# 115 products with no reader, put into half of TensorE's long planned waits

## The chip, the cores and the metric

The kernel runs on one core of a Trainium2 chip. The core has five engines that run their own instruction queues side by side: TensorE (PE: matrix products, and PEld: its weight loads), VectorE (DVE), ScalarE (ACT), GpSimd (POOL) and SyncE (SP, which here issues DMAs). Products land in PSUM, which has banks of 512 fp32 columns on 128 partitions. The metric is the device time of one execution in microseconds; the kernel before is given as the median of nine runs.

## The reference

The input `u` is 8 sequences of 512 tokens with 128 features. Four residual layers follow one another:

```python
x = u
x = x + ssm(layernorm(x))        # tanh/softplus gates, scan over time: z = a*z + b*u_scaled
x = x + linear(layernorm(x))     # one of 8 weight matrices, picked by argmax of logits + Gumbel noise
x = x + delta(layernorm(x))      # 16 heads of size 8, for each t: S += beta*(v - S k) k^T ; o = S q
x = x + moe(layernorm(x))        # 8 experts, top 2 by softmax weight, gelu(x w1 + b1) w2 + b2
```

The delta layer as it stands in the reference is a scan over time, also with a residual of its own inside (it returns `x + scan_out @ w_out + b_out`):

```python
def step(S, inp):
    q_t, k_t, v_t, beta_t = inp
    retrieval = jnp.einsum('bhij,bhj->bhi', S, k_t)
    S = S + jnp.einsum('bhi,bhj->bhij', beta_t * (v_t - retrieval), k_t)
    o_t = jnp.einsum('bhij,bhj->bhi', S, q_t)
    return (S, o_t)
```

## The kernel before, in words

Time is cut into 32 tiles of 16 steps (`QT = 16`); a tile holds 8 sequences x 16 steps = 128 tokens. Eight chunks `g` of four tiles each go through the front layers (`scanned`, `ssm_out`, `linear`, in `first_layers`), through the preparation of the delta rule (`delta_in`), the delta rule itself (`delta_rule`), and the routing (`route`). Groups of one or two chunks (`GROUPS`) then go through the experts (`experts`): tokens are scattered to a table in DRAM by GpSimd (`places`), blocks of 128 rows with one expert each are multiplied by `w1b` into bank `ph`, put through Gelu on ScalarE into `hid`, multiplied by `w2` into a bank `po` or `in`, and gathered back.

The delta rule is the serial part. A tile has four blocks of four steps. For each block VectorE does six instructions in a chain: a multiply of `kq` with the state into `so`, a reduction of `so` into `w`, a multiply with `tmat` into `prod`, a reduction of `prod` into `u_16`, a multiply of keys with it into the block's terms, and a reduction of these into the new state. The state lives in PSUM, in two banks of its own, `st[0]` and `st[1]`, which alternate from block to block; VectorE writes the state after block `n` into the bank of block `n + 1`. In each bank the state and its terms take columns 0 to 319 and `w` columns 320 to 351; `st[1]` also holds `u_16` in columns 352 to 479. Columns 352 to 511 of `st[0]` hold nothing. Before the change only VectorE writes these two banks; ScalarE reads `u_16` into `upd`. Once at the start VectorE clears both.

What each tile's rule needs comes from the other engines: `tmat` and the planes `qkp` from `delta_in`, by products with `head_ones` on TensorE, copies by ScalarE and small steps by GpSimd; `kq` by a DMA from a scratch in DRAM. At the end of a tile TensorE multiplies the planes of `so` and `qkp` with `wo`, and VectorE adds the result to `base`.

PSUM has eight banks here: `st0`, `st1`, `ph0`, `ph1` and four shared ones, `po0`, `po1`, `in0`, `in1`.

All work is recorded first, by `Recorder`, as operations of a `Plan` with an estimated cost each (`_cost`). `place` puts them in order: for each engine in turn it picks among the operations that are ready, by start and by due time, and notes a planned start and end. `best` tries 150 drafts (`DRAFTS`), with due times shaken at random from a fixed seed, and keeps the order with the earliest planned end. `emit` then issues the operations in that order, which the engines' queues keep: each engine executes its own in the order of issue. Semaphore waits between the engines are put in afterwards, from what each operation reads and writes, in the order of issue. `make_identity` writes `ident`, a 128 x 128 identity matrix in SBUF, before the plan's first operation.

In the profile most lines read L317, the line of the recorder's helper; the second product of the experts is L1300, the scatter L1238. So the groups are told apart by tile names.

Of the kernel before, what the change touches and what calls it, by code (L numbers as in the profile page):

```python
# [17 lines left out]
P = 128  # L18
# [52 lines left out]
class Plan:  # L71
# [41 lines left out]
    def add(self, engine, emit, reads, writes, cost, lag=0.0, table=None, group=None):  # L113
        op = Op()
        op.engine, op.emit, op.cost, op.lag, op.table = engine, emit, cost, lag, table
        op.key, op.slack = (self.key, len(self.ops)), self.slack
        op.after, op.begins, op.ends = set(), [], []
        for x in reads:
            self.depend(op, x, False)
        for x in writes:  # L120
            self.depend(op, x, True, group)
        for x in (*reads, *writes):
            if isinstance(x, Bank):
                if x.owner.users == 0:
                    op.begins.append(x.owner)
                if x.owner not in op.ends:
                    x.owner.users += 1
                    op.ends.append(x.owner)
        self.ops.append(op)
# [5 lines left out]
    def later(self, op, f):  # L135
# [4 lines left out]
        if f.engine != op.engine or op.lag < 0:  # L140
            wait += LAG[op.engine] + f.slack
        return wait
# [41 lines left out]
    def best(self):  # L184


        dice, kept = random.Random(1), None
        for draft in range(DRAFTS):
            if draft < len(SWITCH):
                due = {op.key[0]: op.key[0] for op in self.ops}  # L190
                self.switch = SWITCH[draft]
            else:
                due, self.switch = dict(kept[3]), kept[4]
                for key in due:
                    if dice.random() < MOVED:
                        due[key] += dice.gauss(0.0, JITTER)
            for op in self.ops:
                op.rank = due[op.key[0]]
            for turn in range(ROUNDS + 1):
                if turn:  # L200
                    self.backward()
                order, index = self.place()
                end = max(op.end for op in self.ops)
                if kept is None or end < kept[0]:
                    kept = end, order, index, due, self.switch
        for bank, i in kept[2].items():
            bank.index = i
        return kept[1]

    def place(self):  # L210
# [14 lines left out]
        while len(order) < len(self.ops):  # L225
# [40 lines left out]
            for b in op.ends:  # L266
                users[b] -= 1
                if users[b] == 0:
                    banks[index[b]] = done + LAG[op.engine]
            for f in followers[op]:  # L270
                at = done
                if f.engine != op.engine or op.lag < 0:
                    at += LAG[op.engine] + f.slack
                f.ready = max(f.ready, at)
# [4 lines left out]
        return order, index  # L279

    def emit(self):
        kind = mybir.EngineType
        with self.tc.manual_schedule(engines={kind.PE, kind.DVE, kind.Activation, kind.SP}):
            for op, switch in self.best():
                if switch:
                    self.hw.scalar.preload_act_table_set(switch)  # L286
                made = op.emit()
                if op.engine == "gpsimd":
                    self.tc.keep_in_program_order(made)


class Recorder:
# [5 lines left out]
    def __getattr__(self, name):  # L298
        plan, engine = self.plan, self.engine

        def record(*args, group=None, cost=None, **kw):
            def walk(x):
                if isinstance(x, bass.IndirectOffsetOnAxis):
                    return [x.ap]
                return [x] if isinstance(x, (bass.AP, Bank)) else []

            named = [k for k in ("out", "dst", "accum_out") if k in kw]
            outs = [a for k in named for a in walk(kw[k])]
            if not named or named == ["accum_out"]:
                outs += walk(args[0])  # L310
            ins = [a for x in (args if named[:1] in (["out"], ["dst"]) else args[1:]) for a in walk(x)]
            ins += [a for k, x in kw.items() if k not in named for a in walk(x)]

            def emit():
                on = lambda x: x.on(plan.banks) if isinstance(x, Bank) else x
                method = getattr(getattr(plan.hw, engine), name)
                return method(*(on(x) for x in args), **{k: on(x) for k, x in kw.items()})  # L317

            table = next((SETS[x] for x in args if isinstance(x, AF) and x in SETS), None)
            sizes = [_size(x) for x in outs + ins if not isinstance(x, Bank)]  # L320
            n = max([f for _, f in sizes], default=512)
            if "dma" in name:
                whole = min(p * f for p, f in sizes[:2]) if "indirect" not in name else sizes[0][0] * sizes[0][1]
                took, lag = (1.27 if engine == "gpsimd" else 0.42), -4.0 * whole
            else:
                took, lag = _cost(engine, name, n, kw), 0.0
                if ALU.pow in args:
                    took = 0.4 + 0.155 * n
            plan.add(engine, emit, ins, outs, took if cost is None else cost, lag, table, group)
# [32 lines left out]
MOVED = .2  # L362
ROUNDS = 1
LAG = {"tensor": 0.4, "vector": 0.3, "scalar": 0.3, "gpsimd": 0.3, "sync": 0.3}
SWITCH = (3.0, 6.0, 9.0, 12.0)


@with_exitstack
def seq_kernel(
# [42 lines left out]
    hw = tc.nc  # L412
# [22 lines left out]
    def bank(name):  # L435
        return psum.tile([P, N], F32, tag=name, name=name)

    shared = [bank(f"po{i}") for i in range(2)] + [bank(f"in{i}") for i in range(2)]
    nc = Plan(tc, shared)
    own = {t: [bank(f"{t}{i}") for i in range(n)] for t, n in (("ph", 2),)}  # L440

    def ctile(shape, name, dtype=F32):
        return const.tile(shape, dtype, tag=name, name=name)
# [101 lines left out]
    ident = ctile([P, P], "ident")  # L545
# [62 lines left out]
    st = [bank(f"st{i}") for i in range(2)]  # L608
# [8 lines left out]

    u_16 = st[1][:, NS + B * BL : NS + 5 * B * BL].rearrange("p (b t) -> p b t", b=B)

    nc.vector.memset(st[0], 0.0)  # L620
    nc.vector.memset(st[1], 0.0)

# [444 lines left out]
    def route(g, x3, group):  # L1067
# [27 lines left out]
        stat = stile([P, most], "stat")[:, 0:NT]  # L1095
        prob = stile([P, most, NE], "prob")[:, 0:NT]
        by.tensor_sub(prob, best, best[:, :, 0:1].to_broadcast([P, NT, NE]))
        nc.scalar.activation(prob, prob, AF.Exp)
        nc.vector.tensor_reduce(stat, prob, AX.X, ALU.add)
# [480 lines left out]
```

## Time and profile before

| what | value |
|---|---|
| median of 9 runs | 702.34 us (698.95 to 706.26) |
| profiled execution | 703.51 us |
| its span, first to last instruction | 701.7 us |
| mean granted TensorE clock | 0.856 |
| busy: PE, PEld | 513.3 us, 399.1 us |
| busy: DVE, ACT, POOL | 507.5, 458.6, 548.0 us |
| matmul records | 2948 |
| `so<-kq,st`, 128 times | 87.7 us, 685 ns each |

The busy time of an engine is the time in which it executes something, as a share of the span; matmuls are pipelined, and their ends are modelled. The page's second part cuts the span into 40 slices of 17.5 us and gives the busy tenths of each engine, and in the row PEclk the clock that TensorE was granted, in tenths of its full speed. The chain is followed back from the last instruction: at each step to what released it, or to the instruction ahead of it on its engine. In the order of time each row has the start, the duration, the engine, the line, the operation, what it writes and reads, and in brackets the idle time ahead of it with what ended that. In a row of several instructions (x8) the duration runs from the first start to the last end.

### The profile page before, as it was taken

Reading aid. Unit: us, or ns where it says so; the run is one execution under the profiler, and the core shown is the slowest. Engines: PE = TensorE matmul, PEld = TensorE weight load, DVE = VectorE, ACT = ScalarE, POOL = GpSimd, SP = SyncE. Lnnn points to the kernel's source line nnn. Section 1 sums busy time; section 2 is a strip of 40 time slices with the busy share of each in tenths; the row PEclk is TensorE's granted clock in tenths of the full one; section 3 lists DMA queues with packets and bytes.
Section 4 is the critical chain, followed back from the end, with each engine's and each line's share of the span. In section 5 each row is a group of like instructions: output and inputs, shape, how many; then the busy total and the mean of one; then the engine's idle time right before and its main releaser. Section 6 shows DMA issues by size and latency. Waiting matters only on the chain.

```text
span 701.7 us, 10975 instructions
## 1 busy us (share of the span) xinstructions
PE 513.3 (73%) x2948; PEld 399.1 (57%) x2948; DVE 507.5 (72%) x1276; ACT 458.6 (65%) x1054; POOL 548.0 (78%) x681
## 2 busy tenths in 40 slices
PE   5885564766675487788867878739888697897980
PEld 4563123534444245567645666639668687897980
DVE  5673179999999889999989999957999985400013
ACT  4866775756674668897877878736675544664750
POOL 7577575788589979997899998985799888884454
PEclk9957577897787579899988999979899989998995
DMA  3493053253245364655647566554878768568762
GB/s 106 130 284 96 24 133 81 78 150 71 76 98 150 79 187 108 156 151 159 190 119 180 132 175 162 143 165 141 216 204 222 188 192 245 140 198 233 207 192 74
DMA packets 97714, 105.92 MB, mean 151 GB/s; under 512 B 9099, under 2 KB 72534, under 8 KB 97654
## 3 DMA queue, kind: packets, MB, share of 16 engines
q1 hardware_dynamic: 92992, 96.66, 51.3%
q0 software_dynamic: 4160, 8.53, 4.4%
q8 instruction: 25, 0.41, 0.2%
q14 instruction: 35, 0.29, 0.1%
q10 hardware_dynamic: 502, 0.03, 0.0%
HBM read 81.26 MB, written 23.94 MB: 150 GB/s over the span
## 4 chain that ended last, share of the span: by engine, by line
DVE 37%; PE 20%; POOL 19%; ACT 9%; issue 9%; DMA 4%; SPq 1%; POOLq 0%; DVEq 0%; ACTq 0%
DVE st L317 18%; DVE so L317 6%; PE in L317 6%; PE ph L317 6%; PE po L317 4%; POOL b L317 3%; PE po L1300 3%; DVE prod L317 3%; POOL places L1238 3%; POOL f L317 2%; POOL back L317 2%; ACT f L317 2%; DVE x L317 2%; ACT b L317 2%; POOL so L317 2%
## 5 line engine op out<-in xcount | busy, mean ns | idle before, releaser
L317 ACT ACTIVATE hid<-ph,w1b 128x128 f32<-128x128 f32 x396 | 114.1, 377 | 54.2 <-PE ph L317 28.3
L317 PE MATMUL ph<-xbT,w1b 128*128 128x128 f32 x792 | 116.0, 291 | 17.3 <-ACT hid L317 5.8
L317 PEld LDWEIGHTS ph<-xbT,w1b 128*128 128x128 f32 x792 | 106.2, 206 | 25.1 <-ACT hid L317 7.0
L1300 PE MATMUL po<-w_sb,hid 128*128 x632 | 94.6, 289 | 9.9 <-ACT hid L317 7.3
L1300 PEld LDWEIGHTS po<-w_sb,hid 128*128 128x128 f32 x632 | 84.7, 201 | 24.2 <-issue 10.8
L317 DVE TENSOR_TENSOR so<-kq,st 128x512 f32<-128x512 f32 x128 | 87.7, 685 | 9.6 <-PE po L317 3.6
L317 DVE TENSOR_REDUCE st<-so 128x32 f32<-128x288 f32 x128 | 84.2, 658 | 3.3
L317 POOL DMA_INDIRECT back<-results,small_dest x64 | 62.1, 970 | 30.4 <-issue 13.7
L1238 POOL DMA_INDIRECT places<-xne,small_dest x64 | 64.5, 1007 | 19.1 <-issue 13.1
L317 PE MATMUL po<-wo,so 128*128 128x128 f32 x264 | 45.8, 329 | 32.5 <-POOL so L317 14.0
L317 PEld LDWEIGHTS po<-wo,so 128*128 128x128 f32 x264 | 42.8, 240 | 46.8 <-POOL so L317 15.1
L317 DVE TENSOR_REDUCE st<-st 128x64 f32<-128x320 f32 x128 | 63.8, 498 | 4.3
L317 PE MATMUL in<-b,head_ones 128*128 128x512 f32 x80 | 49.6, 709 | 14.9 <-DVE x L317 3.7
L286 ACT ACT_TABLE_LOAD x44 | 56.5, 1283 | 6.1 <-DMA hid<-in_L_ffn_b_dram 5.3
L317 DVE TENSOR_TENSOR st<-kq,st 128x256 f32<-128x256 f32 x128 | 54.8, 428 | 4.2
L317 PE MATMUL in<-b,wqkvb 128*128 128x512 f32 x64 | 44.6, 792 | 13.2 <-DVE x L317 5.4
L317 DVE SCALAR_TENSOR_TENSOR fin<-back,small_weight,fin 128x128 f32<-128x128 f32 x16 | 5.3, 352 | 61.9 <-DMA results<-yb 60.0
L317 PE MATMUL in<-f,wT 128*128 128x512 f32 x64 | 41.3, 735 | 7.4 <-ACT f L317 5.3
L317 POOL TENSOR_TENSOR qkp<-qkp,upd 128x512 f32<-128x512 f32 x32 | 38.9, 1217 | 7.7 <-ACT upd L317 7.5
L317 DVE TENSOR_REDUCE st<-prod 128x32 f32<-128x128 f32 x128 | 37.7, 294 | 7.0 <-ACT upd L317 1.2
L317 POOL TENSOR_TENSOR f<-f,f 128x512 f32<-128x512 f32 x24 | 30.7, 1282 | 12.9 <-ACT f L317 12.9
L317 DVE TENSOR_TENSOR prod<-tmat,st 128x128 f32<-128x128 f32 x128 | 36.6, 286 | 4.3
(287 smaller groups left out, 1242.8 us busy)
## 6 DMA issues: line engine op xcount, KB each, us to landing
kq<-scratch SPq DMA_DIRECT2D x64, 512.0 KB
w1b<-w1b_dram SPq DMA_DIRECT2D x99, 258.0 KB
xb<-places SPq DMA_DIRECT2D x21, 256.0 KB
results<-yb SPq DMA_DIRECT2D x21, 256.0 KB
places<-yb SPq DMA_DIRECT2D x2, 1472.0 KB
x<-in_L_attn_u_dram SPq DMA_DIRECT2D x32, 64.0 KB
w1b_dram<-in_L_ffn_w_dram SPq DMA_DIRECT2D x1, 2048.0 KB
scratch<-qn SPq DMA_DIRECT2D x8, 256.0 KB
```

The lines of the kernel that those rows point to most:

```text
L286: self.hw.scalar.preload_act_table_set(switch)
L317: return method(*(on(x) for x in args), **{k: on(x) for k, x in kw.items()})
L1238: rows_out = hw.gpsimd.indirect_dma_start(out=table[0 : nblk * P, :], out_offset=bass.IndirectOffsetOnAxis(ap=at, axis=0), in_=src, in_off ...
L1300: return hw.tensor.matmul(out_.on(nc.banks), lhsT=src, rhs=w2_f[:, bass.ds(at + c * P, P)], start=(c == 0), stop=(c == NHB - 1),)
```

## The change

`best` keeps, beside the order, each operation's planned start and end. When `emit` comes to a TensorE operation whose planned start lies more than 1.5 us (`GAP`) behind the planned end of the TensorE operation before it, it first issues some extra products: half of the wait (`FILL`) divided by 0.3 us (`FILLER`), rounded down. Over the whole plan these are 115. Each has one column of `ident` as its stationary operand and all of `ident` as its moving one, and writes one row of 128 columns (384 to 511) of `st[0]`, which nothing reads. The extra products are not operations of the plan: the plan's order, its times and the assignment of banks stay as they are.

```diff
                 if kept is None or end < kept[0]:
                     kept = end, order, index, due, self.switch
+                    self.times = {op: (op.start, op.end) for op, _ in order}
...
     def emit(self):
-        kind = mybir.EngineType
+        kind, free = mybir.EngineType, None
         with self.tc.manual_schedule(engines={kind.PE, kind.DVE, kind.Activation, kind.SP}):
             for op, switch in self.best():
+                if op.engine == "tensor":
+
+                    start, end = self.times[op]
+                    if free is not None and start - free > GAP:
+                        for _ in range(int(FILL * (start - free) / FILLER)):
+                            self.filler()
+                    free = end
...
+GAP, FILL, FILLER = 1.5, 0.5, 0.3
...
+    junk = st[0][0:1, 512 - P : 512]
+    nc.filler = lambda: hw.tensor.matmul(junk, lhsT=ident[:, 0:1], rhs=ident, start=True, stop=True)
     nc.vector.memset(st[0], 0.0)
     nc.vector.memset(st[1], 0.0)
```

## The prediction

> **What bounds the kernel now.** I read the page first: the slices, then the chain of work that ended last.
>
> ```profile
> span 701.7 us, 10975 instructions
> ...
> DVE  5673179999999889999989999957999985400013
> ...
> PEclk9957577897787579899988999979899989998995
> ...
> DVE 37%; PE 20%; POOL 19%; ACT 9%; issue 9%; DMA 4%; SPq 1%; POOLq 0%; DVEq 0%; ACTq 0%
> ```
>
> A slice is 17.5 us. From about 100 us to 590 us VectorE is nearly always full, and it holds the largest share of the chain: that is the delta rule (lines `st`, `so`, `prod`), a serial recurrence. TensorE holds a fifth of the chain. Its granted clock is low mostly in the first half. Next, busy time by stretch:
>
> ```profile
> core 0: us, PE busy (x) PEld busy (x) DVE busy (x) ACT busy (x) POOL busy (x), PEclk, DMA share, GB/s
> ...
> 52.00:105.00 53.00, 32.81 (x79) 13.79 (x79) 21.27 (x48) 39.27 (x63) 36.34 (x48) 0.69 0.33 87
> 105.00:290.00 185.00, 119.91 (x512) 80.59 (x512) 169.39 (x390) 123.24 (x221) 148.57 (x187) 0.80 0.43 110
> 290.00:420.00 130.00, 106.25 (x605) 80.60 (x604) 119.44 (x285) 104.68 (x226) 119.05 (x146) 0.89 0.59 158
> 420.00:702.00 282.00, 216.46 (x1604) 194.58 (x1602) 163.04 (x422) 159.71 (x452) 208.77 (x243) 0.91 0.66 183
> ```
>
> Between 105 and 290 VectorE works 169 of 185 us, TensorE 120. So TensorE's time is cheap there and VectorE's is dear. Before 105, where no delta rule runs yet, no engine is full and the chain hops between them; one stretch of it runs wholly at half clock:
>
> ```profile
> 62.90:90.20 27.30, 16.36 (x31) 6.72 (x31) 3.38 (x5) 19.14 (x35) 17.82 (x22) 0.50 0.12 32
> ```
>
> The last view is the order of time, for two things. First, one product's price at half and at full clock, from two rows of eight records, which are four products each (an fp32 product leaves two records; the page has 792 for the 396 products of `ph`):
>
> ```profile
> 66.49 2.08 PE L317 MATMUL in<-wsel,f 128*128 128x128 f32 x8 [0.68 <-ACT f L317]
> ...
> 654.89 1.06 PE L317 MATMUL ph<-xbT,w1b 128*128 128x128 f32 x8
> ```
>
> Second, what a reader of a PSUM bank waits for. The four products of one `hid` write four disjoint quarters of bank `ph`, and the first Gelu reads only the first quarter:
>
> ```profile
> 640.06 1.91 PE L317 MATMUL ph<-xbT,w1b 128*128 128x128 f32 x8
> ...
> 642.06 1.14 ACT L317 ACTIVATE hid<-ph,w1b 128x128 f32<-128x128 f32 x4 [6.69 <-PE ph L317]
> ```
>
> It starts at 642.06, 0.09 us after the last of the four (641.97), not after the first, though ScalarE had been idle for 6.69 us. In this program waits are placed by bank, not by column.
>
> **The change, part by part.** *Where the products go.* The plan's own start and end times (used here for order alone, not for time) have 28 TensorE waits over 1.5 us, 77.6 us in sum; half of each, cut into 0.3 us and rounded down, is 115 products. Nine waits with 48 products begin before the delta rule is two tiles old (plan 52.9 to 120.1), sixteen with 57 lie between 146 and 284, three with 10 at 362, 366 and 409. None lies in the last 290 us.
>
> *What each does.* It loads one column of `ident`, streams `ident`'s 128 columns and writes row 0, columns 384 to 511, of `st[0]`. No row shows a one-column load. The cheap end is 0.22 us, from the chain's piece of 16 back-to-back records at 575.73 (1.79 us); the dear end is 0.52, the half-clock row. I take 0.265 at full clock and 0.52 at half, from the two rows above, since there too the loads run beside the matmuls.
>
> *What waits for what.* `st[0]` is the bank in which the delta rule keeps its state. By the row above, a product waits for the last VectorE instruction on `st[0]` that stands ahead of it in the plan's order, and VectorE's next one on `st[0]` waits for the last product of the group. A group is emitted after everything planned to start before the TensorE instruction behind the wait, so the VectorE instruction ahead of it is one that starts just before the wait ends: the products run at the end of the wait, not in it. The tenth group, four products ahead of the `head_ones` product at 148.24, shows it:
>
> ```profile
> 148.24 1.10 PE L317 MATMUL in<-b,head_ones 128*128 128x512 f32 x2 [0.26 <-ACT f L317]
> ...
> 150.93 0.43 DVE L317 TENSOR_TENSOR st<-kq,st 128x256 f32<-128x256 f32 x1
> 151.39 0.50 DVE L317 TENSOR_REDUCE st<-st 128x64 f32<-128x320 f32 x1
> ```
>
> Today TensorE runs 2.7 us ahead of the plan's place here. Then the group waits until 151.36, and the reduction of 151.39 waits for four products.
>
> *VectorE's price.* I laid all 28 groups against the trace in this way. In seven, VectorE's next instruction on `st[0]` follows at once, and the group's time goes into the recurrence (the clock is that granted at that place):
> - 4 products behind 99.95, next 100.66, half clock: 2.08
> - 4 behind 150.93, next 151.39, full: 1.06
> - 4 behind 163.08, next 163.80, half; 0.43 us of other VectorE work lies between: 1.65
> - 4 behind 171.44, next 171.91, full: 1.06
> - 3 behind 287.31, next 288.03, half: 1.56
> - 4 behind 369.78, next 370.37, half: 2.08
> - 3 behind 372.71, next 373.17, half: 1.56
>
> That is 11.05 us, and two handovers of 0.09 us each time, less the usual 0.03 between two VectorE instructions: 7 x 0.15 = 1.05. Sum +12.1; with all at full clock 7.5. Six of the seven lie where the chain is VectorE's own; at 287 it runs through ScalarE and the transposes at 286.44, which would wait for the same group until about 289.7 instead, so that place pays either way. In the other seventeen groups after 97 us the next `st[0]` instruction is 1.5 to 4.3 us off, and the recurrence's work on the other bank covers the products; without it they would cost 0.265 to 0.52 each. At half clock the two groups of seven (behind 110.39 and 123.23, next 112.94 and 126.33) would overrun by 1.6 together, which goes to the range; the six behind 233.14 overrun where the chain is GpSimd's. The four groups at the front come below.
>
> *TensorE's own delay.* The product behind each such group starts late against VectorE: by 6 us at 96.40 (its group waits for the `so` multiply of 99.95), 4 at 148.24, 3 at 169.99 and 226.00, 1 to 2 elsewhere. Queued behind it are all later products, ScalarE's copies and GpSimd's steps on them. I cost it at nothing: after 96.40 TensorE has waits of 1.58 and 3.69, ScalarE of 2.51 and 4.48, GpSimd of 3.84 before the end of tile 0. Without that cover it costs what is left of the delay; the nearest limits are `tmat`, ready 2.57 us before its multiply at 156.91, and the linear layer's product, 0.74 us before the add at 168.65. From 0 to +6.
>
> *The clock.* Before the delta rule `st[0]` is free, and 25 products (3, 6, 12, 4) really run in waits, ahead of 59.78, 64.18, 73.67 and 79.69. The low stretches last multiples of 3.41 us. The one from 62.93 follows a 3.41 us in which TensorE worked 1.1 us; six products would make that 2.7. If they count as work, the transposes at 64.18 take 0.73 (the row at 113.88) instead of 1.63, the `wsel` products about 0.5 less, and the `head_ones` product at 79.69 takes 1.12 (57.88) instead of 2.08, with ScalarE idle behind it: -2.4. The rest of 73 to 85 is covered by ScalarE, busy without a break. If they do not count, 12 products at 0.52 end at 74.8 and 4 at 80.4, past the 73.67 and 79.69 they stand before: +1.8. I take -2.4, since every low stretch of this trace up to 690 us ends after 3.41 us in which TensorE worked over 2.8. In the delta rule I expect no gain: the products come when the wait is nearly over, and TensorE idles first as before.
>
> [...]
>
> **Sum.** +12.1 - 2.4 = +9.7. The profiled execution took 703.51 with a span of 701.7; the median of nine is 702.34. The change is added to the median: 712.0.
>
> **Rivals.**
> - *No wait on the bank* (faster): tracking by column lets the products run in the waits. For it: nobody reads those columns. Against: 642.06. Only the clock's 2.4 remains, up to 5 if later stretches profit: 697 to 700. It decides if VectorE's rows show no new wait.
> [...]
> - *The delay spreads*: ScalarE and GpSimd, held behind late products, keep VectorE waiting once more: +4 to +8, 716 to 720. For it: the 0.74 us. Against: the waits at 105 to 114.
>
> **How the numbers follow.** Forecast 0.60 (707 to 716: bounds 7.5 and 12.1, -2.4 and +1.8), spread 0.22, clock repays 0.10, no wait 0.08. A measurement tells about 0.3% (2.1 us) from no change. Faster: 0.08 and a third of the clock's case, 0.11; same, half of that case and 0.01 of the forecast, 0.06; slower 0.83. The range leaves out most of the no-wait case and the far end of the spread: 702 to 720.
>
> **What would show it.** VectorE waits of 1 to 2 us, ended by TensorE on `st`, at the seven places; TensorE waits ended by VectorE before the new rows; the products of the first four groups inside waits, and PEclk above 0.50 between 63 and 80. VectorE's busy time must stay at 507 us. It is wrong if the new rows start right behind the TensorE row ahead of them in the delta rule, or if GpSimd's chain at 200 to 240 does not move with VectorE's.

## The result and the profile after

The changed kernel takes 708.25 us (median of 10 runs, 705.56 to 714.2), the kernel before in the same comparison 702.33 us (31 runs). The ratio on record is 1.0109 with a 95% interval of 1.0082 to 1.0136, that is +7.7 us (5.8 to 9.6); the two medians lie 5.9 us apart, at the lower end of that. The change makes the kernel slower, by an amount that is known to about 2 us. The profiled execution took 708.48 us with a span of 706.8; before it was 703.51 and 701.7. TensorE's mean granted clock rose from 0.856 to 0.884 while the time grew.

The page of the changed kernel: the span, the slices of VectorE and of the granted clock, the chain by engine, and the group of the products (the helper's line is now L325, the products are L630).

```profile
span 706.8 us, 11448 instructions
...
DVE  5673159988899789899997999975999996300013
...
PEclk9957868898897599999998999988998999999995
...
PE 8%; DVE 3%; DMA 2%; issue 1%; POOL 1%; ACT 1%; POOLq 0%; SPq 0%; ACTq 0%; DVEq 0%
...
L630 PE MATMUL st<-ident 128*1 128x128 f32 x230 | 41.2, 341 | 42.7 <-DVE st L325 28.4
```

All 230 records of the 115 products are there. They keep TensorE busy for 41.2 us, and TensorE sits idle 42.7 us ahead of them, 28.4 of it for VectorE's work on `st`. The chain of this page is followed back only over a sixth of the span (its shares sum to 16%), so its shares can't be set beside those of before. VectorE's row is still nearly full from 100 to 590 us. Its busy time went from 507.5 to 505.2 us.

Busy time by stretch, the same stretches and columns as in the prediction, and the low-clock stretch of the front:

```profile
52.00:105.00 53.00, 37.05 (x128) 17.33 (x128) 20.45 (x44) 36.08 (x60) 33.77 (x46) 0.76 0.36 92
105.00:290.00 185.00, 137.99 (x653) 87.96 (x653) 165.37 (x386) 119.34 (x215) 146.16 (x180) 0.83 0.41 107
290.00:420.00 130.00, 100.29 (x619) 74.15 (x618) 117.27 (x284) 105.92 (x223) 117.87 (x151) 0.97 0.56 150
420.00:702.00 282.00, 223.48 (x1633) 201.37 (x1633) 168.67 (x435) 164.78 (x467) 215.09 (x248) 0.92 0.69 188
...
62.90:90.20 27.30, 19.82 (x81) 9.30 (x79) 4.32 (x8) 20.50 (x36) 17.63 (x22) 0.81 0.10 29
```

Between 105 and 290 TensorE works 18 us more and VectorE 4 us less (165.4 for 169.4): VectorE's missing time is new idle time. The clock rose in every stretch, most between 62.9 and 90.2, from 0.50 to 0.81.

The waits by who waits for whom (engine, tile, releaser: sum in us, times, longest):

```profile
PE st L630 <- DVE st L325: 28.4, 15, 5.0
...
DVE st L325 <- PE st L630: 10.1, 9, 2.0
```

The kernel before has neither. The second line, with one more wait of 1.5 us ahead of a multiply into `so`, is what the change makes VectorE wait: ten waits, 11.65 us. The first place of the seven shows it in the order of time:

```profile
102.48 0.68 DVE L325 TENSOR_TENSOR so<-kq,st 128x512 f32<-128x512 f32 x1
103.21 1.87 PE L630 MATMUL st<-ident 128*1 128x128 f32 x8 [6.94 <-DVE so L325]
105.00 2.08 PE L325 MATMUL in<-wT,f 128*128 128x128 f32 x8
105.11 0.66 DVE L325 TENSOR_REDUCE st<-so 128x32 f32<-128x288 f32 x1 [1.96 <-PE st L630]
```

VectorE's multiply ends at 103.16; four products (eight records) start 0.05 us later, after TensorE has been idle for 6.94 us. VectorE's reduction starts 0.03 us after the last of them and has waited 1.96 us. Before, it followed the multiply at once. The products write columns that no one reads; both engines wait all the same.

Where in the profile the time is lost and won can be followed by one and the same VectorE instruction in each trace. The table gives its start, as a difference to the kernel before (worked out from the orders of time; the four kernels of the right ran on one chip):

```
start before, and what it is             after   seven_only  without_seven  own_bank  one_each
 59.52  x<-in,gain,x (no product yet)    +2.8    +1.1        -1.0           -0.7      -1.3
 91.98  b<-b,beta                        +1.7    +1.1        -3.4           +0.2      -1.3
 99.95  first so<-kq,st                  +2.5    +1.3        -0.9           +0.6      -1.4
171.44  st<-kq,st                        +7.4    +6.4        -1.0           +0.7      +0.1
250.61  so<-kq,st                        +6.0    +6.4        -2.8            0.0       0.0
306.05  st<-prod                         +6.1    +6.3        -3.8           +1.9      -0.5
369.78  st<-st                           +3.9    +5.6        -4.3           +1.1      -1.6
535.19  st<-so                           +7.3    +9.1        -4.2           +2.2      -0.3
```

The first row stands ahead of every product, so its -1.3 to +2.8 is what two executions differ by at the start; a row is to be read against it.

### The profile page after: what moved, and what is told of

Read it like the earlier page. It is cut to its first block, busy times and chain, and to the rows that moved or that the text cites. A ratio compares the mean times of both kernels' runs of the same rounds, so it can differ in the third digit from the quotient of the medians.

```text
span 706.8 us, 11448 instructions
## 1 busy us (share of the span) xinstructions
PE 536.1 (76%) x3178; PEld 410.3 (58%) x3178; DVE 505.2 (71%) x1276; ACT 456.9 (65%) x1054; POOL 547.5 (77%) x681
## 5 line engine op out<-in xcount | busy, mean ns | idle before, releaser
L325 ACT ACTIVATE hid<-ph,w1b 128x128 f32<-128x128 f32 x396 | 113.9, 376 | 53.4 <-PE ph L325 25.1
L325 PE MATMUL ph<-xbT,w1b 128*128 128x128 f32 x792 | 115.4, 290 | 11.1 <-DMA w1b<-w1b_dram 4.2
L325 PEld LDWEIGHTS ph<-xbT,w1b 128*128 128x128 f32 x792 | 105.5, 205 | 19.1 <-ACT hid L325 6.0
L1311 PE MATMUL po<-w_sb,hid 128*128 x632 | 93.1, 286 | 8.4 <-ACT hid L325 6.2
L1311 PEld LDWEIGHTS po<-w_sb,hid 128*128 128x128 f32 x632 | 83.2, 198 | 21.5 <-issue 9.9
L325 DVE TENSOR_TENSOR so<-kq,st 128x512 f32<-128x512 f32 x128 | 87.7, 685 | 8.5 <-PE st L630 1.5
L325 DVE TENSOR_REDUCE st<-so 128x32 f32<-128x288 f32 x128 | 84.3, 659 | 6.1 <-PE st L630 2.9
L325 POOL DMA_INDIRECT back<-results,small_dest x64 | 62.0, 969 | 29.9 <-issue 14.5
L630 PE MATMUL st<-ident 128*1 128x128 f32 x230 | 41.2, 341 | 42.7 <-DVE st L325 28.4
L325 DVE TENSOR_REDUCE st<-st 128x64 f32<-128x320 f32 x128 | 63.8, 498 | 9.6 <-PE st L630 4.7
L325 DVE TENSOR_TENSOR st<-kq,st 128x256 f32<-128x256 f32 x128 | 54.8, 428 | 6.6 <-PE st L630 2.5
L630 PEld LDWEIGHTS st<-ident 128*1 128x1 f32 x230 | 20.6, 99 | 66.8 <-DVE st L325 36.1
L325 PEld LDWEIGHTS po<-wo,so 128*128 128x128 f32 x264 | 37.1, 213 | 28.4 <-POOL so L325 15.0
L325 PE MATMUL in<-b,head_ones 128*128 128x512 f32 x80 | 48.0, 689 | 7.3 <-DVE x L325 1.7
L325 PE MATMUL po<-wo,so 128*128 128x128 f32 x264 | 40.3, 300 | 16.3 <-POOL so L325 12.8
L325 DVE SCALAR_TENSOR_TENSOR fin<-back,small_weight,fin 128x128 f32<-128x128 f32 x16 | 5.4, 352 | 59.6 <-DMA w1b<-w1b_dram 56.9
L325 PE MATMUL in<-b,wqkvb 128*128 128x512 f32 x64 | 37.9, 679 | 10.7 <-DVE x L325 5.5
L325 DVE TENSOR_REDUCE st<-prod 128x32 f32<-128x128 f32 x128 | 37.7, 294 | 7.6 <-ACT upd L325 1.1
L325 POOL TENSOR_TENSOR f<-f,f 128x512 f32<-128x512 f32 x24 | 31.4, 1309 | 15.1 <-ACT f L325 14.9
L325 POOL TENSOR_TENSOR qkp<-qkp,upd 128x512 f32<-128x512 f32 x32 | 38.5, 1204 | 5.5 <-ACT upd L325 5.3
```

The costliest lines, as they stand in the source:

```text
L630: nc.filler = lambda: hw.tensor.matmul(junk, lhsT=ident[:, 0:1], rhs=ident, start=True, stop=True)
L1311: return hw.tensor.matmul(out_.on(nc.banks), lhsT=src, rhs=w2_f[:, bass.ds(at + c * P, P)], start=(c == 0), stop=(c == NHB - 1),)
```

## The experiments

Groups are numbered 1 to 28 in the order of the plan; the seven of the prediction are 5, 10, 12, 13, 25, 26 and 27. Each edit is one of the changed kernel; lines left out are marked by `...`. Four kernels ran on a first chip; the other eight ran in two sets of four on other chips, on which the kernel before took 745.1 us, so that only ratios to the kernel before in the same set are compared. The kernel before has a profile from the first comparison alone.

### The seven groups alone, and all but the seven

```diff
+STALLS = (5, 10, 12, 13, 25, 26, 27)
...
-                        for _ in range(int(FILL * (start - free) / FILLER)):
+                        wait += 1
+                        for _ in range(int(FILL * (start - free) / FILLER) if wait in STALLS else 0):
```

> Only the 26 products of the seven groups behind which VectorE's next instruction on `st[0]` follows at once (the 5th, 10th, 12th, 13th, 25th, 26th and 27th wait); the other 89 are left out. Theory W (VectorE is made to wait for the bank): the seven places cost VectorE 9.75 us in the profile of the changed kernel, so about +8 to +10 on 702.3: 710 to 712, with seven VectorE waits of 0.9 to 2.0 us ended by TensorE on `st`. Theory O (each product costs by occupying TensorE's queue, wherever it stands): 26 of 115 products bear 26/115 of the 7.6 us, 1.7: 704.

> The other 89 products alone, the seven groups left empty. W: what is left is the front's gain of clock (about -1 to -2.4) and one VectorE wait of 1.4 us behind the 20th wait, where the chain is GpSimd's: 699 to 702. O: 89 of 115 products bear 5.9 us: 708.

The second kernel has `if wait not in STALLS`. The 26 products of the seven groups alone cost all that the change costs: 710.07 us, ratio 1.0104 (1.0085 to 1.0123), +7.3 us. The other 89 make the kernel faster on this chip: 699.31 us, ratio 0.9958 (0.9940 to 0.9976), -2.9 us. VectorE's waits, first with the seven groups only:

```profile
DVE st L326 <- PE st L632: 9.6, 6, 2.0
...
DVE so L326 <- PE st L632: 1.3, 1, 1.3
```

and without them:

```profile
DVE st L326 <- PE st L632: 1.6, 2, 1.4
```

Seven waits of 10.9 us against two of 1.6. So the cost hangs on where in VectorE's order a group stands, not on how many products there are in all. The two prices sum to +4.4 us (+5.0 by the medians), the whole change measured +7.7 (5.8 to 9.6; +5.9 by the medians). In the profiles, from the row of 59.52 to that of 535.19, the parts give +8.0 and -3.2 and the whole +4.5. So the parts add up by the profiles and nearly by the medians; why the ratio of the whole stands higher, no run says.

### One product in each of the 28 places

```diff
-                        for _ in range(int(FILL * (start - free) / FILLER)):
+                        wait += 1
+                        for _ in range(1 if True else 0):
```

> One product in each of the 28 waits instead of half a wait full. W, with the stall as handover plus products one after another: seven times 0.1 to 0.15 plus one product of 0.23 to 0.5, 2.5 to 4.5 us in sum, and no gain at the front: 704.5 to 706.5. If the handover itself were the price, whatever the number of products: seven times 1.4, 711. O: 28/115 of 7.6 is 1.9: 704.

It took 701.37 us, ratio 0.9993 (0.9971 to 1.0015): no difference, where a loss was expected. VectorE does wait, at six of the seven places (not at 163), for 0.47 to 0.68 us each, 3.3 in sum, as here:

```profile
98.56 0.68 DVE L326 TENSOR_TENSOR so<-kq,st 128x512 f32<-128x512 f32 x1
99.30 0.58 PE L631 MATMUL st<-ident 128*1 128x128 f32 x2 [6.03 <-DVE so L326]
99.92 0.66 DVE L326 TENSOR_REDUCE st<-so 128x32 f32<-128x288 f32 x1 [0.68 <-PE st L631]
```

One product, 0.58 us long, makes this place wait 0.68; four, 1.87 us long, made it 1.96: the wait is some 0.1 us of handover and the products' own length. In the table the kernel has lost 1.5 us between the rows of 99.95 and 171.44 and won as much again by 369.78. The loss is there. Of what is won back, 1.7 us are VectorE instructions that ran shorter than in the kernel before; the other three experiments of this chip show 2.6 to 3.1 there, whichever products they have, so the run doesn't show that the products pay for it.

### The same products, issued behind the TensorE instruction ahead of the wait

```diff
...
+                        if wait in EARLY:
+                            behind[last] = int(FILL * (start - free) / FILLER)
...
                 made = op.emit()
+                for _ in range(behind.get(op, 0)):
+                    self.filler()
...
+EARLY, LATE = (5, 10, 12, 13, 25, 26), ()
```

> Six of the seven groups (without the 27th wait), 23 products, each issued right behind the TensorE instruction ahead of its wait instead of right ahead of the one behind it: same products, same bank, same waits in the plan, only another place among VectorE's instructions. Laid against the trace of the kernel before, the groups of waits 5, 12, 25 and 26 then end before VectorE's next instruction on `st[0]`; wait 10 costs 0.7 and wait 13 costs 1.2. W: 1.9 us and two handovers, about 2.2, so 703 to 705, with VectorE waits ended by TensorE on `st` at two places. If the products' place does not matter (O, or a price per product): at the end of the waits the same six cost 9.4 us of VectorE waits in the run with the seven alone, of which 7.3 x 9.4/10.97 = 6.3 reached the time: 708 to 709.

> Only the 23 products of groups 5, 10, 12, 13, 25, 26, where the change puts them. Theory (VectorE waits for the bank at these six places, 1.3 to 2.0 us each, nothing else changes): the six waits of seven_only sum to 9.4 us, ratio 1.008 to 1.0125. Rival (the loss of seven_only hangs on its seventh group, or on that chip): below 1.005.

> The same 23 products of groups 5, 10, 12, 13, 25, 26, each group issued behind the TensorE instruction ahead of the wait instead of before the one behind it. Theory (only the place in VectorE's order costs, not the products): no VectorE wait ended by these products over 0.5 us at the six places but those where VectorE's state instruction still follows closely, ratio 0.998 to 1.004, that is 0.6 to 1.2% below six_late on the same chip. Rival (the products cost wherever they stand): within 0.3% of six_late.

`six_early` gave 0.9997 (0.9970 to 1.0025). Since it ran on another chip than the seven late groups, the pair was run again on one chip: late 751.43 us, ratio 1.0091 (1.0055 to 1.0126); early 746.25 us, ratio 1.0025 (0.9998 to 1.0053). The same 23 products cost 5.2 us more in the later place. Group 10, late:

```profile
151.82 0.43 DVE L339 TENSOR_TENSOR st<-kq,st 128x256 f32<-128x256 f32 x1
...
152.31 1.09 PE L645 MATMUL st<-ident 128*1 128x128 f32 x8 [3.42 <-DVE st L339]
...
153.43 0.50 DVE L339 TENSOR_REDUCE st<-st 128x64 f32<-128x320 f32 x1 [1.18 <-PE st L645]
```

and early:

```profile
148.58 0.43 DVE L339 TENSOR_TENSOR st<-kq,st 128x256 f32<-128x256 f32 x1
...
148.62 1.03 PE L645 MATMUL st<-ident 128*1 128x128 f32 x8
...
149.69 0.50 DVE L339 TENSOR_REDUCE st<-st 128x64 f32<-128x320 f32 x1 [0.68 <-PE st L645]
```

Late, TensorE waits 3.42 us for the state's bank and then VectorE waits for TensorE. Early, TensorE is free at 148.6 and the products run at once, beside a VectorE instruction that isn't on this bank; of the group's 1.03 us VectorE waits 0.68. Over all six places VectorE waits 9.2 us late and 1.5 us early. The products and the bank are the same, so what costs is the place in the order in which the bank's users are issued. The late place also holds up the TensorE instruction behind the group; how much of the 5.2 us goes that way the pair doesn't tell apart.

### Most of the change, with four of the seven moved ahead

```diff
+EARLY = (5, 12, 25, 26)
+LATE = tuple(i for i in range(29) if i not in (5, 10, 12, 13, 25, 26, 27))
```

> The run without the seven, plus the groups of waits 5, 12, 25 and 26 issued at the start of their waits, where the recurrence does not meet them: 104 products. W: no VectorE wait is added to that run; the clock may hold in a few more stretches: 698 to 700.5. O: 15 products more cost 1: 700.5.

The best of both was hoped for, 698 to 700.5 us on the first chip, and it missed: 748.74 us, ratio 1.0041 (1.0021 to 1.0061), +3.1 us. Moving a group ahead helps only if TensorE is on time there. Group 11, late, holds TensorE until 160.6, and group 12, moved ahead, stands behind it:

```profile
158.79 1.87 PE L645 MATMUL st<-ident 128*1 128x128 f32 x8 [3.93 <-DVE st L339]
...
160.59 1.83 PE L339 MATMUL po<-wo,qkp 128*128 128x128 f32 x8
...
162.26 0.60 PE L339 MATMUL in<-ident,f 128*128 128x128 f32 x4
162.79 1.03 PE L645 MATMUL st<-ident 128*1 128x128 f32 x8
...
163.86 0.50 DVE L339 TENSOR_REDUCE st<-st 128x64 f32<-128x320 f32 x1 [2.60 <-PE st L645]
```

VectorE's reduction, which comes after group 12 in the order of issue, now waits 2.60 us for it; in `six_late`, without a group 11, the wait at group 12 was 1.44 us. Here TensorE's own delay, which I had costed at nothing, costs VectorE. That this one wait is all of the miss isn't shown.

### Each group in the bank of the product behind it

```diff
-    junk = st[0][0:1, 512 - P : 512]
+    def filler(out_):
...
+            whole = shared[out_.owner.index]
...
+        hw.tensor.matmul(whole[0:1, 512 - P : 512], lhsT=ident[:, 0:1], rhs=ident, start=True, stop=True)
```

> Products at the same places and of the same size, but into the PSUM bank that the TensorE instruction behind the wait is going to write anyway, so that they add no wait on VectorE's bank; the 11th and the 13th wait, which lie within a sum in PSUM, stay empty: 107 products in 26 waits. W: no VectorE wait on `st` ended by TensorE; the products run as soon as the bank is free, most of them in the wait: 698 to 702.5, below 702.3 by what the clock gives. O: 7.1 us as before, 708 to 710.

Here `whole` is the bank that the TensorE instruction behind the wait writes. 107 of the products go there instead of into the state's bank (groups 11 and 13 stay empty, since the product behind them adds to a sum). It took 704.78 us, ratio 1.0036 (1.0015 to 1.0057), +2.5 us, and fitted neither expectation. VectorE doesn't wait for products at all. But a product now waits for the last reader of that bank, runs late again, and holds up the real product behind it:

```profile
78.66 1.86 PE L637 MATMUL in<-ident 128*1 128x128 f32 x8 [2.07 <-ACT kn L326]
...
80.44 1.94 PE L326 MATMUL in<-b,head_ones 128*128 128x512 f32 x2
```

Here `kn` ends at 78.60 and `head_ones` starts at 80.44, 1.84 us later; before, it started at 79.69, 0.05 us behind the end of `kn` at 79.64. The front's gain doesn't come (row of 91.98 in the table: +0.2, `without_seven` -3.4). A second such place, three products at 287.79 that waited 0.98 us for ScalarE on `qkp`, lies where the table goes from 0.0 to +1.9. So it isn't enough here that VectorE is spared: at these two places the products in the bank of the next TensorE instruction had that bank's wait ahead of themselves, 2.07 and 0.98 us, and behind the first of them the queue was longer by their 1.86 us.

### Where the gain of the other 89 comes from

The condition under which a group is issued, in the line of the first experiment:

```
front_only:       if wait <= 4
waits_20_21:      if wait in (20, 21)
without_seven_b:  if wait not in (5, 10, 12, 13, 25, 26, 27)
without_nine:     if wait not in (5, 10, 12, 13, 20, 21, 25, 26, 27)
```

> The 25 products of the first four waits alone, all before the delta rule. The prediction's step: the clock holds and 2.4 us come back: 699.9. Theory G (the gain arrives but is used up before the delta rule starts: in the run without the seven, VectorE's first step on `tmat` starts 2.2 us earlier against the start-up, yet the delta rule no earlier, since the small VectorE steps in between take longer beside GpSimd's): 701.5 to 702.8.

> Nine products alone, of the 20th and 21st wait, between two stretches of the delta rule where the chain is GpSimd's and TensorE's. Theory C (they lift the clock for the products of 238 to 250, which run at half clock before): the two products with `f` and `head_ones` and the two with `wqkvb` of that stretch take 1.1 instead of 2.07, the VectorE waits at 240 and 250 shrink by 1 us each, and one wait of 1.4 us at 234 is covered: 699.5 to 701. If the gain of the run without the seven came from the front instead: 702 to 703.

> The same 89 products as without_seven (all groups but 5, 10, 12, 13, 25, 26, 27), to see whether its gain comes back on another chip. Theory (the price of the change is the seven stalls alone, the rest of the products lift the clock): ratio 0.993 to 0.998, as the 0.9958 measured before. Rival (the 0.9958 belonged to that chip): 0.9985 to 1.003.

> As without_seven_b, also without the nine products of groups 20 and 21 (plan order ahead of the tail of GpSimd's chain near 233 us). Theory (the gain of without_seven comes mostly from the clock at 236 to 250 us, which these products lift): 0.25 to 0.45% slower than without_seven_b, ratio to the kernel before 0.998 to 1.001. Rival (the gain is spread over the groups, or is the front's): within 0.15% of without_seven_b.

```
                 products  ratio   95% interval
front_only       25        0.9967  0.9942 to 0.9993
waits_20_21       9        1.0020  0.9993 to 1.0046
without_seven_b  89        0.9985  0.9956 to 1.0014
without_nine     80        1.0005  0.9974 to 1.0037
```

Groups 20 and 21 were thought to bring most of the gain, since the changed kernel's VectorE makes up time just there. They don't by themselves (1.0020, where 0.996 to 0.998 would have been it), and the last two kernels can't be told apart. The gain of the 89 is also not established on this other chip: -0.15%, with no change inside the interval. `front_only`, on a third chip, is faster by its ratio, by as much as the prediction's 2.4 us would make it (0.9966); its median lies only 0.2 us below that of the kernel before, and its profile, as shown below, has lost the gain again before the delta rule. So by time it stays open what the front is worth.

On the same VectorE instructions as in the table `without_seven_b` goes from +2.9 at 99.95 to +0.1 at 306.05, 2.8 us won, as much as on the first chip (-0.9 to -3.8); `without_nine` wins 1.9 there and `waits_20_21` 0.6. Not all of this is the products': `seven_only`, which has none of the 89, wins 3.1 us over these rows if its waits for products are left out. What is theirs can be told at three VectorE waits, ahead of the rows that stand at 240.27, 241.50 and 250.61 in the kernel before: together 3.3 us there. They shrink by

```
2.3 to 2.4   changed kernel, without_seven, without_seven_b, four_moved
1.3          waits_20_21
0.8          without_nine
0.3          own_bank
0.0 to 0.1   seven_only, one_each, six_late, six_early, six_early_b, front_only
```

So the products do speed up this place, by 2.3 us in the kernels that have the 89, and groups 20 and 21 bring somewhat over half of it. But all eight kernels of these chips then lose 41 to 47 us against the first chip's kernel before, nearly all of it after 535 us. There `front_only`'s VectorE sits idle for 73 us ahead of `fin`, by its profile until a transfer of weights (`w1b<-w1b_dram`) lands; in the changed kernel it is 57. Whether that end swallows the gain, or the gain was partly the first chip's, stays open.

What the clock does at the front is clear. The stretch from 62.90 to 90.20, `seven_only` (no product there), then `without_seven`:

```profile
62.90:90.20 27.30, 16.11 (x32) 6.63 (x30) 3.38 (x5) 19.42 (x36) 17.81 (x22) 0.50 0.10 30
```

```profile
62.90:90.20 27.30, 19.77 (x69) 9.16 (x70) 5.01 (x7) 21.09 (x39) 18.98 (x20) 0.87 0.20 52
```

In the kernel before, too, the clock there is 0.50. With groups 1 to 4 it is 0.75 in `own_bank` and `front_only`, 0.81 in the changed kernel and 0.87 in `without_seven`. With one product in each it isn't lifted: over 52 to 105 it is 0.70 in `one_each`, 0.69 in the kernel before and 0.76 to 0.88 in these four. `without_seven` reaches `b<-b,beta` at 88.57 instead of 91.98: of these 3.4 us 1.0 is the start of the execution, and 2.4 the products'. Then it gives 2.5 back before the delta rule starts. From `b<-b,beta` to the first `so` VectorE has an unbroken row of small steps; it takes 8.0 us in the kernel before and 10.5 here. One of these steps, in `without_seven`:

```profile
97.53 2.71 POOL L326 TENSOR_TENSOR both<-f,f 128x512 f32<-128x512 f32 x2 [1.50 <-ACT f L326]
97.77 1.34 DVE L326 TENSOR_TENSOR tmat<-b,beta 128x128 f32<-128x128 f32 x1
```

and in the kernel before:

```profile
99.64 0.39 DVE L317 TENSOR_TENSOR tmat<-b,beta 128x128 f32<-128x128 f32 x1
...
100.24 2.49 POOL L317 TENSOR_TENSOR both<-f,f 128x512 f32<-128x512 f32 x2 [2.35 <-ACT f L317]
```

The same instruction takes 0.39 us when GpSimd is idle beside it and 1.34 beside a GpSimd multiply; the `tmat` of 128x256 takes 0.61 in the changed kernel at 100.32, with GpSimd idle, and 1.70 in `without_seven` at 94.80, beside a GpSimd multiply. Having come earlier, VectorE meets GpSimd's work. `front_only` repeats it on another chip: 1.6 us won between the first two rows of the table, 3.1 lost to the third. The other four kernels with groups 1 to 4 in the state's bank do it too: each wins 0.5 to 2.3 us between the first two rows and loses 0.9 to 3.3 to the third; in the six kernels without these groups, or with one product in each, the three rows stay within 0.15 us of each other. That the neighbour makes the step long is read from these rows; no run took GpSimd's work away.

## Why the prediction was right, point by point

The forecast was 712.0 us, range 702 to 720, with 0.83 on slower. Measured were 708.25 us: the direction, the mechanism of the loss and its places were right, the size was 9.7 us for a measured 7.7 (5.8 to 9.6). Two of the terms that make the size were wrong, the front by 2.1 us and the clock in the delta rule by 2.3; these errors have opposite signs and cancel, so that the sum still lies near is partly luck.

- *Waits go by bank.* Right. Products on columns that nobody reads stop VectorE and are stopped by it (28.4 and 10.1 us in the waits above), and `six_late` beside `six_early_b` shows that the order of issue on the bank decides. The rival without a wait on the bank is refuted.
- *The products run at the end of the wait.* Right at the seven places: TensorE is idle ahead of each, for 6.94 us at 103.21, 3.35 at 155.97 and 0.91 at the last. Four of the other groups in the delta rule (6, 8, 21 and 22) do start right behind the TensorE row ahead of them, which the prediction had named as a sign of being wrong; none of them is among the seven.
- *The seven places.* All seven are there, and three more waits: 1.41 us at 243.00 and, at the two groups of seven that the prediction had put into the range with 1.6, 0.31 at 117.75 and 0.18 at 131.37. The term was mis-sized: predicted +12.1, measured 1.96, 1.60, 1.10, 1.13, 0.91, 1.52 and 1.53, which is 9.75 us (10.97 in `seven_only`). Two of the parts were too dear. A product was priced by a row with 128-column loads, 0.265 and 0.52 us; four back-to-back ones take 1.03 to 1.09 at full clock and 1.87 at half, some 0.25 and 0.46 each (granted 1.00 at 164.76, 0.50 at 103.21). And five of the seven had been put at half clock, as the trace of before granted it there. But the clock's changes lie elsewhere in the changed kernel: with their handovers the places of 163, 287 and 369 us, granted 0.63, 1.00 and 0.70 over their products, cost 1.10, 0.91 and 1.52 instead of 1.80, 1.71 and 2.23, and the one of 151 us, put at full clock and granted 0.64, 1.60 instead of 1.21. The one of 372 us, still at half clock, costs 1.53 instead of 1.71.
- *TensorE's own delay costs nothing.* Held in the changed kernel where the stalls lie close: from 99.95 to 171.91 (before) its VectorE falls back from +2.5 to +8.5, by 6.0 us, and its six waits for products there sum to 6.3. At 243 the text had named the group as one that overruns under GpSimd's chain, and had put it at nothing; it costs 1.41. In `four_moved` and `own_bank` the same kind of delay did cost, so the upper end of +6 was rightly kept.
- *The front, -2.4.* The clock rose as predicted, and `without_seven` shows the 2.4 at 88.57. But the changed kernel itself, from the row of 59.52 to that of 91.98, gains 1.1 only (+2.8 to +1.7). Its `wsel` products bring 0.9 instead of 0.5, the transposes 0.15 instead of 0.9, and `head_ones` still runs at half clock, 2.08 us, behind four products that start it 0.36 us later. The next step failed too, by the profiles: I took time won at the front as time won at the end. It is used up in VectorE's small steps before the delta rule (0.9 of the 1.1 here, 2.5 of the 2.4 in `without_seven`). The ratio of `front_only`, 0.9967, speaks against this, its profile for it.
- *No clock gain in the delta rule.* Wrong: this term was missing. At 240 to 247 us of the changed kernel it shows how:

```profile
240.24 2.72 PE L630 MATMUL st<-ident 128*1 128x128 f32 x12 [2.56 <-DVE prod L325]
242.99 1.12 PE L325 MATMUL in<-ident,b 128*128 128x128 f32 x4
244.03 1.33 PE L630 MATMUL st<-ident 128*1 128x128 f32 x6
245.29 1.13 PE L325 MATMUL in<-f,wT 128*128 128x512 f32 x2
```

Both groups run at half clock, 0.45 and 0.44 us a product. The granted clock is 0.50 from 240.00 to 245.13 and 1.00 from there to 251.90, and the `in<-f,wT` behind the second group takes 1.13 us; before, it took 2.07 at 238.24, at a granted 0.50. So at this place products that come late in their wait have the full clock behind them. The last of the three VectorE waits named above, before and after:

```profile
250.61 0.69 DVE L317 TENSOR_TENSOR so<-kq,st 128x512 f32<-128x512 f32 x1 [1.92 <-PE po L317]
...
256.57 0.69 DVE L325 TENSOR_TENSOR so<-kq,st 128x512 f32<-128x512 f32 x1 [0.89 <-PE po L325]
```

The term is 2.3 us, by the runs with and without these products. From 171.44 to 369.78 the changed kernel's VectorE comes back by more, from +7.4 to +3.9 although it waits 3.5 us more for products at 180, 243 and 295 us, 6.9 in all; but the rest isn't shown to be the products'. 2.9 us are VectorE instructions that run shorter than in the kernel before, and in `seven_only`, without the other groups, they run shorter by 3.1. 1.5 us are a wait at 357.84, which shrinks as much in `front_only`, whose last product lies 280 us earlier: there the granted clock differs with no product near (`in<-b,wqkvb` at 353.96 took 2.08 us before, at 0.50, and takes 1.13 at 359.39, at 1.00, with no product in the 60 us ahead of it). The chance of 0.10 for a clock that repays the stalls stood on an estimate that no run shows; what the runs show in the delta rule is 2.3 us, and the sign stayed.

The sum, from single executions: +9.75 and +1.9 for the waits, -0.3 for the front up to the first `so`, -2.3 for the clock at 240 us, -2.9 for VectorE's shorter instructions and -1.5 for the wait at 357.84, some +4.6 us; the table shows +4.5 by 535 us, if the late start of +2.8 is left out. The medians stand 5.9 us apart, the ratio says +7.7 (5.8 to 9.6). What makes the difference of 1 to 3 us, no run settles. Had the waits gone by column, the 12.1 would have fallen away and the forecast been 699.9; the waits of 28.4 and 10.1 us on columns that nobody reads decide for the bank.

## What to carry to other kernels

A scratch write isn't free because nobody reads it: in this program waits go by bank, so it takes its place in the order of everyone who uses that bank, and where the bank's next user followed at once its price was its own length plus a tenth of a microsecond (1.87 us of products, 1.96 of wait). The same filler cost less right behind the instruction ahead of the gap, where the engine was on time (1.5 us of VectorE's waits against 9.2 at six places); `own_bank` and `four_moved` (+2.5 and +3.1 us) show that neither sparing one engine nor moving single groups was enough. A bank with no other user, which this kernel doesn't have, was not tried. And time won ahead of a serial stage is to be followed to the start of that stage before it is counted: of the 2.4 us won at the front in `without_seven` nothing was left there.

## What the runs showed of the hardware

- Products with a one-column stationary operand (four took 1.03 us at 164.76, at a granted 1.00) went with a higher granted clock: over 62.90 to 90.20 it was 0.50 in the kernel before and in `seven_only`, and 0.75, 0.75, 0.81 and 0.87 in `own_bank`, `front_only`, the changed kernel and `without_seven`, which have groups 1 to 4.
- A VectorE step of 128x128 fp32 operands took 0.39 us with GpSimd idle and 1.34 beside a GpSimd multiply (two rows, no experiment); the delta rule's own steps keep their durations (`so<-kq,st` 685 ns in the mean, before and after).
- Two other chips ran the same kernel before in 745.1 us instead of 702.3. Where it lost the time there wasn't profiled; the changed kernels lost it near the end: `front_only` stands 0.7 us behind the first chip's kernel before at 306 us, 3.7 at 535 us and 41.7 at its last VectorE instruction.
